# Expert blocks: gather by channel quarters, and a 32x32 block transpose on VectorE in place of TensorE transposes

## The chip, the cores and the metric

The kernel runs on one core of a Trainium2 chip. The metric is device microseconds of one execution, from three runs of the kernel before: 2274.1, 2275.79 and 2278.2 us, median 2275.79. Smaller is better. The engines have short names in the profile: PE is TensorE, DVE VectorE, ACT ScalarE, POOL GpSimd, SP SyncE.

## The reference

Two layers work on x of 4 sequences x 512 positions x 512 channels, in float32. Each layer has a first half (a WKV gate, then a token mixer: a Mamba2 block in layer 0, causal attention in layer 1) and a second half (a second WKV gate, then a feed-forward part: a mixture of experts in layer 0, a ternary FFN in layer 1); each half is added to x. The change lies in the mixture of experts:

```
logits = x @ gate_w.T + gate_b
top_vals, top_idx = jax.lax.top_k(logits, TOP_K)          # 2 of 8 experts
routing = jax.nn.softmax(top_vals, axis=-1)
for e in range(E):
    h = x @ w1[e].T + b1[e]                               # 512 -> 2 * 512
    x_glu, x_lin = h[:, 0::2], h[:, 1::2]
    y = x_glu * jax.nn.sigmoid(1.702 * x_glu) * (x_lin + 1.0)
    out = out + (y @ w2[e].T + b2[e]) * jnp.sum(routing * (top_idx == e), axis=-1)[:, None]
```

## The kernel before

The kernel is written in a tile framework: its scheduler puts the instructions of each engine in one order, and each engine then works through its own queue in that order, waiting on semaphores. The stages follow each other and overlap at their edges: the first WKV gates (0 to some 42 us), the Mamba2 block (to some 660 us), the experts (659 to 1134 us), attention (to about 2000 us), and the last FFN.

**Routing.** The gated rows of all 2048 tokens are written to a DRAM tensor `rows_h` (a row of 512 floats per token). The function `route` (L527) ranks the experts for every token and counts, with a triangular matrix `tri_lt` as matmul weight (L553), the place of each token within its expert; it also builds `toks`, a 128x128 table of tokens by place. `order_blocks` (L648 to L707) then makes blocks of 128 tokens of one expert: a matmul with `toks` gives the token of each lane of each block, and a few small DVE operations turn it into row indices, `idx_h` to gather with and `idx_o` to scatter with, and into the expert of a block, `eb`. It is called twice. The first call (L1433), before the last sequence is routed, orders 17 blocks (`NEARLY`); the second (L1525) orders the rest. 39 blocks are possible, 37 always run (`ALWAYS`), and the last two sit under a condition; 37 ran in the profiled execution.

**A block.** Class `Experts` does one block per round (`round`, L864), as a pipeline over three blocks:

- `fetch` (L766): one indirect DMA from POOL's queue (L770) gathers 128 rows of 2048 bytes into `hb` (128 partitions x 512 channels, three buffers). Fetches run `LOOK` = 3 blocks ahead, and a new one needs the buffer that a flip has freed.
- `flip` (L776): four PE transposes of 128x128 into a PSUM tile `pfl` (L782), and an ACT copy (L784) to `hT` (channels on partitions, two buffers).
- `first_half` (L806): four matmuls `pg` (L811), a bias add on DVE (`g`, L816), a tanh on ACT; four matmuls `pn` (L822), three DVE operations (L826 for g, L828 and L829 for u).
- `finish` (L832): four PE transposes `pyt` (L835) of u and an ACT pass to `yT` (L837).
- `down` (L840): four matmuls `po` (L844), a bias add to `o` (L849) and an indirect DMA that scatters the rows (L850).

A float32 matmul shows as two records in the profile, so a group of four has eight. PE's order in a steady round is pg of block i, pyt and po of earlier blocks, pfl of block i + 1, pn of block i.

**Weights.** `w1` lies in DRAM as `w1x`, laid out on the host (`_lay_out`, L1951) so that partition p of contraction part k holds channel 128 k + p. SP's queue loads each expert's halves ahead of the block.

**What stands beside it.** Between the rounds the program issues pieces of the next layer's WKV gates: scans of 1.2 us each on DVE (L259, L265), divisions, and ACT activations with table loads between them. At the edge to the stage before, the last Mamba2 work is still there: a multiply of y and the gate z on POOL (L1214), and a DVE operation `rs` (L1242) that waits for it. At the kernel's start POOL makes constants (iotas, triangular masks) and the skip multiplies (L957), while DVE runs the first WKV scans.

Of the kernel before, what the change touches and what calls it, by code (L numbers as in the profile page):

```python
# [18 lines left out]
P = 128  # L19
B, T, C = 4, 512, 512  # L20
NC = C // P
# [9 lines left out]
E, I = 8, 512  # L31
# [13 lines left out]

HEADS, GROUPS, KVC = 16, 4, 128
HPG = HEADS // GROUPS
SCALE = KVC ** -0.5
MASKED = -1.0e30

# [33 lines left out]
def block_kernel(ctx: ExitStack, tc: tile.TileContext, a: dict, out: bass.AP):  # L84
    nc = tc.nc
# [60 lines left out]
    def ps_tp(name):  # L146
        return ps.tile([P, 512], F32, tag="tp", name=name, bufs=2)
# [263 lines left out]
    def gated(l, b, xb, pool, part=slice(0, T), **kw):  # L411
# [25 lines left out]
    tri_lt = rt.tile([P, P], F32, name="tri_lt")  # L437
    nc.gpsimd.affine_select(out=tri_lt, in_=ones, compare_op=ALU.is_gt, fill=0.0, base=0,
                            pattern=[[1, P]], channel_multiplier=-1)
# [34 lines left out]
    e_nq = count("e_nq", [[NQ, E]])  # L474
    v_id = count("v_id", [[1, 1]], 1)

    v_lo = rt.tile([P, 1], F32, name="v_lo")
    v_e = rt.tile([P, 1], F32, name="v_e")
# [48 lines left out]
    def route(lg, b, fine, pool, **kw):  # L527
# [22 lines left out]
            yield  # L550
        pc = ps_tp("pcnt")
        mm_ = m.rearrange("p t e -> p (t e)")
        nc.tensor.matmul(pc[:, :n], lhsT=tri_lt, rhs=mm_, start=True, stop=True)  # L553
# [86 lines left out]


    taken = rt.tile([P, 1], F32, name="taken")
    idx_h = rt.tile([P, NBLK], I32, name="idx_h")
    idx_o = rt.tile([P, NBLK], I32, name="idx_o")
    eb = rt.tile([1, NBLK + 1], I32, name="eb")
    in_use = eb[:, NBLK:]
# [1 line left out]
    def order_blocks(lo, hi):  # L648

        n = hi - lo  # L650
        cv = rt.tile([P, 1], F32, tag="cv", name="cv")
        nc.vector.tensor_tensor(jk, sel, cnt[:, (N2 if lo else N2 - NT), :], ALU.mult)
        nc.vector.tensor_reduce(cv, jk, AX.X, ALU.add)
        use = rt.tile([P, 1], F32, tag="use", name="use")
        if lo == 0:
            nc.vector.scalar_tensor_tensor(use, v_lo, float(P), cv, ALU.add, ALU.is_le)
        else:
            nc.vector.tensor_tensor(use, v_lo, cv, ALU.is_lt)
            nc.vector.tensor_tensor(use, use, taken, ALU.subtract)
        pi = ps_tp("pidx")  # L660
        rank = rt.tile([P, 1], F32, tag="vrank", name="vrank")
        if lo == 0:
            nc.tensor.matmul(pi[:, P : P + 1], lhsT=tri_lt, rhs=use, start=True, stop=True)
            nc.vector.tensor_copy(rank, pi[:, P : P + 1])
        else:

            two = rt.tile([P, 2], F32, tag="two", name="two")
            nc.vector.tensor_tensor(jk, sel, cnt[:, NT, :], ALU.mult)
            nc.vector.tensor_reduce(rank, jk, AX.X, ALU.add)
            nc.vector.tensor_scalar(two[:, 0:1], v_lo, rank, use, ALU.is_lt, ALU.mult)  # L670
            nc.vector.tensor_tensor(two[:, 1:2], use, two[:, 0:1], ALU.subtract)
            nc.tensor.matmul(pi[:, P : P + 2], lhsT=tri_lt, rhs=two, start=True, stop=True)
# [7 lines left out]
            nc.vector.scalar_tensor_tensor(  # L680
                rank, pi[:, P : P + 1], two[:, 0:1], rank, ALU.mult, ALU.add
            )
        if lo == 0:
# [8 lines left out]
        gf = tmp.tile([P, NBLK], F32, tag="th", name="gf")  # L692
        nc.vector.tensor_scalar(gf[:, :n], pi[:, :n], NROW - 2.0, None, ALU.add)
        nc.vector.tensor_copy(idx_h[:, lo:hi], gf[:, :n])
        low = tmp.tile([P, NBLK], I32, tag="th", name="low")
        nc.vector.tensor_scalar(
            low[:, :n], idx_h[:, lo:hi], T - 1, (B - 1) * T, ALU.bitwise_and, ALU.bitwise_xor
        )
        nc.vector.tensor_scalar(
            idx_h[:, lo:hi], idx_h[:, lo:hi], 1, (B - 1) * T,  # L700
            ALU.logical_shift_right, ALU.bitwise_and,
        )
        nc.vector.tensor_tensor(idx_h[:, lo:hi], idx_h[:, lo:hi], low[:, :n], ALU.bitwise_xor)
        ef = tmp.tile([1, NBLK], F32, tag="th", name="ef")
        nc.vector.tensor_scalar(ef[:, :n], pi[0:1, 2 * P : 2 * P + n], E - 1.0, None, ALU.add)
        nc.vector.tensor_copy(eb[:, lo:hi], ef[:, :n])
        nc.vector.tensor_copy(idx_o[:, lo:hi], pi[:, :n])  # L707

    class Experts:
# [56 lines left out]
        def fetch(self, i):  # L766
            if i >= self.known or i in self.hb:
                return
            hb = self.sm.tile([P, C], F32, tag="hb", name="hb", bufs=3)
            nc.gpsimd.indirect_dma_start(  # L770
                out=hb, out_offset=None, in_=rows_h[: (B if i >= NEARLY else B - 1) * T, :],
                in_offset=bass.IndirectOffsetOnAxis(ap=idx_h[:, i : i + 1], axis=0),
            )
            self.hb[i] = hb

        def flip(self, i):  # L776
            if i in self.hT or i not in self.hb:
                return
            hb = self.hb[i]
            pt = ps_tp("pfl")  # L780
            for k in range(NC):
                nc.tensor.transpose(pt[:, k * P : (k + 1) * P], hb[:, k * P : (k + 1) * P], ident)  # L782
            hT = self.sm.tile([P, NC, P], F32, tag="hT", name="hT", bufs=2)
            nc.scalar.copy(hT.rearrange("p k t -> p (k t)"), pt)  # L784
            self.hT[i] = hT

        def weights(self, i, early=False):
# [764 lines left out]
    with att as ph:  # L1552
# [15 lines left out]
            )  # L1568
            return wd

        SQ, SLOTS = 32, 13
        QUAD = P // SQ
# [350 lines left out]
def _lay_out(n):  # L1923
# [24 lines left out]
        "gate_b": n["L0_ffn_gate_b"],  # L1948
    }
    by_part = lambda v: v.reshape(E, -1, P, v.shape[-1]).swapaxes(1, 2)  # L1950
    w1x = np.stack([by_part(t(w1[:, i::2, :])) for i in range(2)], 2)  # L1951
    got = {
        "cols": np.concatenate([cols[k] for k, _ in _COLS], 1),
        "rows": np.concatenate([np.asarray(rows[k]) for k, _ in _ROWS]),
# [35 lines left out]
```

## Time and profile before

| what | value |
|---|---|
| runs shown | 2274.1, 2275.79, 2278.2 us |
| the profiled execution's own time | 2278.28 us |
| its span (first to last instruction) | 2276.6 us |
| mean granted TensorE clock | 0.98 |
| PE busy | 2134.7 us |
| DVE busy | 1524.0 us |
| ACT busy | 972.2 us |
| POOL busy | 417.2 us |
| packets of under 512 B, of all | 14592 of 112452 |

The profile is of one execution. "Busy" is the time in which an engine has an instruction running. A group line names the source line, engine, operation, output and inputs, then busy us, mean ns of one, then the idle time of the engine just ahead of these instructions and what ended it. A timeline line gives start, duration, and in brackets the idle time before and what ended it. PE's matmuls overlap in the pipeline, so the distance between starts tells what a group costs. "Clock" is the share of full speed that TensorE was granted.

### The profile page before, as it was taken

How to read it: one execution, taken by the hardware profiler on the slowest of the kernel's cores; microseconds unless marked ns; L12 is line 12 of the kernel's file. 1: busy time of each engine (PE TensorE's matmuls, PEld its weight loads, DVE VectorE, ACT ScalarE, POOL GpSimd, SP SyncE). 2: the span in 40 equal slices, each digit the busy share in tenths (PEclk: the TensorE clock that was granted, in tenths of full speed). 3: DMA queues.
4: the chain of work that ended last, by engine and by line, in shares of the span. 5: the costliest groups of instructions: out<-in, count | busy, mean ns of one | idle time of the engine just before them, and what ended most of it. 6: DMA issues, size and time to landing. Idle time of an engine off the chain costs nothing. (4 is left out here: it accounts for less than half of the span.)

```text
span 2276.6 us, 23890 instructions
## 1 busy us (share of the span) xinstructions
PE 2134.7 (94%) x7528; PEld 1226.5 (54%) x7528; DVE 1524.0 (67%) x3041; ACT 972.2 (43%) x1900; POOL 417.2 (18%) x558
## 2 busy tenths in 40 slices
PE   2879999999999999999989999999999999999998
PEld 1545565555655444444444455555555555568887
DVE  8698989989642665566567766566667765456332
ACT  4476666766732233233254434333333333243222
POOL 4023232421332111111211111111111111100000
PEclk9889989999999999999999999999999999999999
DMA  7542341432523548978675566446545464441100
GB/s 261 169 141 75 102 158 66 153 121 65 186 76 136 190 164 298 341 273 277 209 249 179 172 191 186 139 138 190 167 143 158 139 196 142 131 184 38 37 19 20
DMA packets 112452, 357.38 MB, mean 157 GB/s; under 512 B 14592, under 2 KB 23168, under 8 KB 102912
## 3 DMA queue, kind: packets, MB, share of 16 engines
q1 hardware_dynamic: 87584, 277.26, 36.0%
q0 software_dynamic: 22432, 74.34, 11.1%
q10 hardware_dynamic: 2304, 4.20, 0.5%
q8 instruction: 62, 1.02, 0.2%
q14 instruction: 70, 0.57, 0.1%
HBM read 337.91 MB, written 108.00 MB: 196 GB/s over the span
## 5 line engine op out<-in xcount | busy, mean ns | idle before, releaser
L1661 POOL DMA_DIRECT2D turned<-turned x248 | 135.4, 552 | 713.7 <-DVE turned L1653 435.6
L1615 PE MATMUL pq<-h,wq 128*128 128x512 f32 x512 | 235.4, 597 | 2.0 <-DVE h L404 1.7
L1717 PE MATMUL pd<-cx,wd 128*128 128x512 f32 x512 | 223.3, 594 | 0.0
L128 ACT ACTIVATE pr<-psc,nmax 128x128 f32<-128x128 f32 (+3 forms) x256 | 134.7, 526 | 168.9 <-DVE nmax L1642 168.3
L1048 PE MATMUL pc<-h,wxb 128*128 128x512 f32 x320 | 148.6, 620 | 44.3 <-DVE h L1307 39.2
L1637 PE MATMUL psc<-kT,qT 128*128 128x128 f32 (+3 forms) x512 | 158.2, 442 | 14.5 <-ACT pr L128 14.5
L1702 PE MATMUL pctx<-pT,v 128*128 128x512 f32 (+3 forms) x512 | 153.3, 443 | 13.7 <-DMA pT<-turned 13.3
L1640 DVE TENSOR_TENSOR psc<-psc,mask 128x128 f32<-128x128 f32 x256 | 70.4, 283 | 140.5 <-PE psc L1637 140.3
L1717 PEld LDWEIGHTS pd<-cx,wd 128*128 128x128 f32 x512 | 96.5, 191 | 115.3 <-issue 110.1
L1702 PEld LDWEIGHTS pctx<-pT,v 128*128 128x128 f32 x512 | 98.1, 193 | 98.0 <-issue 67.0
L1615 PEld LDWEIGHTS pq<-h,wq 128*128 128x128 f32 x512 | 94.4, 192 | 100.9 <-issue 93.7
L811 PE MATMUL pg<-w,hT 128*128 128x512 f32 x296 | 136.0, 601 | 6.9 <-ACT hT L784 6.8
L844 PE MATMUL po<-w,yT 128*128 128x512 f32 x296 | 135.9, 600 | 6.2 <-ACT yT L837 6.2
L822 PE MATMUL pn<-w,hT 128*128 128x512 f32 x296 | 133.3, 592 | 0.0
L1725 DVE TENSOR_TENSOR xr<-xr,pd 128x512 f32<-128x512 f32 x64 | 43.8, 685 | 126.6 <-PE pd L1717 126.6
L1637 PEld LDWEIGHTS psc<-kT,qT 128*128 128x128 f32 x512 | 86.2, 192 | 73.6 <-ACT pr L128 31.1
L1048 PEld LDWEIGHTS pc<-h,wxb 128*128 128x128 f32 x320 | 61.8, 198 | 116.4 <-issue 74.5
L1642 DVE TENSOR_REDUCE nmax<-psc 128x1 f32<-128x128 f32 (+3 forms) x256 | 122.7, 480 | 1.9
L1653 DVE STREAM_TRANSPOSE turned<-pr 128x128 f32<-128x128 f32 x248 | 120.8, 498 | 1.4
L1710 ACT COPY cx<-pctx 128x512 f32<-128x512 f32 x64 | 37.2, 581 | 187.5 <-PE pctx L1702 187.5
L1119 PE MATMUL pz<-wzt,h 128*128 128x512 f32 x256 | 115.2, 598 | 0.3 <-ACT st L1220 0.3
L1267 PE MATMUL po<-wot,yT 128*128 128x512 f32 x256 | 115.2, 604 | 0.0
(343 smaller groups left out, 4198.0 us busy)
## 6 DMA issues: line engine op xcount, KB each, us to landing
w<-in_w1x SPq DMA_DIRECT2D x76, 1024.0 KB
turned<-turned POOLq DMA_DIRECT2D x248, 208.0 KB, 3.9
pT<-turned SPq DMA_DIRECT2D x62, 832.0 KB
w<-in_w2x SPq DMA_DIRECT2D x38, 1024.0 KB
wb<-in_b1x SPq DMA_DIRECT2D x38, 512.0 KB
lm<-cs SPq DMA_DIRECT2D x32, 512.0 KB
kt<-in_fT SPq DMA_DIRECT2D x62, 256.0 KB
ek<-ek SPq DMA_DIRECT2D x62, 256.0 KB
```

The source lines that it names most:

```text
L128: nc.scalar.activation(*args, **kw)
L811: nc.tensor.matmul(pg, lhsT=hT[:, k, :], rhs=self.w1[s][0][:, k, :], start=(k == 0), stop=(k == NC - 1))
L822: nc.tensor.matmul(pn, lhsT=hT[:, k, :], rhs=self.w1[s][1][:, k, :], start=(k == 0), stop=(k == NC - 1))
L844: nc.tensor.matmul(po, lhsT=yT[:, j, :], rhs=self.w2[s][:, j, :], start=(j == 0), stop=(j == NI - 1))
L1048: nc.tensor.matmul(pc, lhsT=wxb[:, k, m * P : (m + 1) * P], rhs=h[:, k, :], start=(k == 0), stop=(k == NC - 1),)
L1615: nc.tensor.matmul(pq, lhsT=u.wq[:, k, i * KVC : (i + 1) * KVC], rhs=u.h[:, k, :], start=(k == 0), stop=(k == NC - 1),)
L1637: nc.tensor.matmul(psc[:, :n], lhsT=qT[:, qi * P : n], rhs=u.kT[:, :n], start=True, stop=True)
L1642: nc.vector.tensor_reduce(nmax, psc[:, :n], AX.X, ALU.max, negate=True)
L1653: nc.vector.transpose(blocks[:, :, 3 * qi : 4 * qi + 1, :].rearrange("p c k j -> p k c j"), pr)
L1661: nc.gpsimd.dma_start(out=d[:, :, r].rearrange("c i s -> i c s"), in_=blocks[r * SQ : (r + 1) * SQ].rearrange("i c k j -> i c (k j)"),)
L1702: nc.tensor.matmul(pctx[:, kj * P :].rearrange("p (q r j) -> p q r j", r=QUAD, j=SQ), lhsT=u.v[:, kj, :], rhs=pT[:, :, 4 * kj : 10 + kj : ...
L1717: nc.tensor.matmul(po, lhsT=dense_w[u.g][:, i, m * P : (m + 1) * P], rhs=u.ctxT[i], start=(i == 0), stop=(i == HPG - 1),)
```

## The change

The gather becomes four indirect DMAs per block. The rows in DRAM are seen as 8192 quarters of 128 channels (512 bytes). Partition p takes channel quarter p // 32, and the r-th DMA brings, for the 32 tokens 32 r to 32 r + 31, one quarter to each of four groups of 32 partitions: `hb` is now [128, 4, 128]. One DVE transpose, which turns each 32x32 block within its group of 32 partitions, then gives `hT` with channels on partitions and all 128 tokens side by side. The channel on partition p of part k is thus not 128 k + p but 128 (p // 32) + 32 k + p % 32, and the host lays out `w1x` in that order. PE's transposes and ACT's copy go.

The indices are four times as many: `order_blocks` makes a widened copy of `toks` (each group of 32 columns repeated four times, 128x512, on DVE), four matmuls with it, and arithmetic on [128, 4, n] instead of [128, n], and then puts the quarter's number in the low two bits. The number is made once, by an iota on POOL and a DVE operation. `tri_lt` is dropped: `route` uses `tri_gt`, which the Mamba2 block has already (tokens of a tile are then counted from the other end), and `order_blocks` uses `tri_le` and subtracts the diagonal, `use`. `v_lo` and `v_e` become columns of one tile.

```
-    idx_h = rt.tile([P, NBLK], I32, name="idx_h")
+    idx_h = rt.tile([P, QUAD, NBLK], I32, name="idx_h")
+    quarter = rt.tile([P, 1], I32, name="quarter")
+    nc.gpsimd.iota(quarter, pattern=[[1, 1]], base=0, channel_multiplier=1)
+    nc.vector.tensor_scalar(
+        quarter, quarter, 5, QUAD * (B - 1) * T, ALU.logical_shift_right, ALU.bitwise_xor
+    )
...
+        wide = tmp.tile([P, QUAD, QUAD, SQ], F32, tag="th", name="wide")
+        nc.vector.tensor_copy(
+            wide,
+            toks.rearrange("p (r j) -> p r j", r=QUAD).unsqueeze(2).to_broadcast([P, QUAD, QUAD, SQ]),
+        )
+        for r in range(QUAD):
+            nc.tensor.matmul(
+                pi[:, 3 * P + r * n : 3 * P + (r + 1) * n],
+                lhsT=wide[:, r].rearrange("p q j -> p (q j)"),
+                rhs=of[:, :n], start=True, stop=True,
+            )
...
+        nc.vector.tensor_scalar(
+            low, ih, 2, QUAD * (T - 1), ALU.logical_shift_left, ALU.bitwise_and
         )
         nc.vector.tensor_scalar(
+            ih, ih, 1, QUAD * (B - 1) * T, ALU.logical_shift_left, ALU.bitwise_and
         )
+        nc.vector.tensor_tensor(ih, ih, low, ALU.bitwise_xor)
+        nc.vector.tensor_tensor(
+            ih, ih, quarter.unsqueeze(2).to_broadcast([P, QUAD, n]), ALU.bitwise_xor
+        )
...
-            hb = self.sm.tile([P, C], F32, tag="hb", name="hb", bufs=3)
-            nc.gpsimd.indirect_dma_start(
-                out=hb, out_offset=None, in_=rows_h[: (B if i >= NEARLY else B - 1) * T, :],
-                in_offset=bass.IndirectOffsetOnAxis(ap=idx_h[:, i : i + 1], axis=0),
-            )
+            hb = self.sm.tile([P, QUAD, NC * SQ], F32, tag="hb", name="hb", bufs=3)
+            quarters = rows_h[: (B if i >= NEARLY else B - 1) * T, :].rearrange(
+                "r (q c) -> (r q) c", q=QUAD
+            )
+            for r in range(QUAD):
+                nc.gpsimd.indirect_dma_start(
+                    out=hb[:, r, :], out_offset=None, in_=quarters,
+                    in_offset=bass.IndirectOffsetOnAxis(ap=idx_h[:, r, i : i + 1], axis=0),
+                )
...
-            pt = ps_tp("pfl")
-            for k in range(NC):
-                nc.tensor.transpose(pt[:, k * P : (k + 1) * P], hb[:, k * P : (k + 1) * P], ident)
             hT = self.sm.tile([P, NC, P], F32, tag="hT", name="hT", bufs=2)
-            nc.scalar.copy(hT.rearrange("p k t -> p (k t)"), pt)
+            nc.vector.transpose(
+                hT.rearrange("p k (r j) -> p r k j", r=QUAD), hb.rearrange("p r c -> p (r c)")
+            )
...
-    by_part = lambda v: v.reshape(E, -1, P, v.shape[-1]).swapaxes(1, 2)
-    w1x = np.stack([by_part(t(w1[:, i::2, :])) for i in range(2)], 2)
+    by_part = lambda v: v.reshape(E, -1, P, v.shape[-1]).swapaxes(1, 2)
+    by_quad = lambda v: v.reshape(E, QUAD, NC, SQ, -1).swapaxes(2, 3).reshape(E, P, NC, -1)
+    w1x = np.stack([by_quad(t(w1[:, i::2, :])) for i in range(2)], 2)
```

More of the change, by code (lines that the diff above doesn't have):

```diff
@@ L47 @@
 HPG = HEADS // GROUPS
+SQ = 32
+QUAD = P // SQ
 SCALE = KVC ** -0.5
@@ L435, in block_kernel @@
                             pattern=[[1, E], [-1, E]], channel_multiplier=0)
-    tri_lt = rt.tile([P, P], F32, name="tri_lt")
-    nc.gpsimd.affine_select(out=tri_lt, in_=ones, compare_op=ALU.is_gt, fill=0.0, base=0,
-                            pattern=[[1, P]], channel_multiplier=-1)
     sel = rt.tile([P, E], F32, name="sel")
@@ L475, in block_kernel @@
     v_id = count("v_id", [[1, 1]], 1)
-    v_lo = rt.tile([P, 1], F32, name="v_lo")
-    v_e = rt.tile([P, 1], F32, name="v_e")
+    v_both = rt.tile([P, 2], F32, name="v_both")
+    v_lo, v_e = v_both[:, 0:1], v_both[:, 1:2]
     jk = rt.tile([P, E], F32, name="jk")
@@ L552, in route @@
         mm_ = m.rearrange("p t e -> p (t e)")
-        nc.tensor.matmul(pc[:, :n], lhsT=tri_lt, rhs=mm_, start=True, stop=True)
+        nc.tensor.matmul(pc[:, :n], lhsT=tri_gt, rhs=mm_, start=True, stop=True)
         nc.tensor.matmul(pc[:, n : 2 * n], lhsT=ones, rhs=mm_, start=True, stop=True)
@@ L662, in order_blocks @@
         if lo == 0:
-            nc.tensor.matmul(pi[:, P : P + 1], lhsT=tri_lt, rhs=use, start=True, stop=True)
-            nc.vector.tensor_copy(rank, pi[:, P : P + 1])
+            nc.tensor.matmul(pi[:, P : P + 1], lhsT=tri_le, rhs=use, start=True, stop=True)
+            nc.vector.tensor_tensor(rank, pi[:, P : P + 1], use, ALU.subtract)
         else:
@@ L671, in order_blocks @@
             nc.vector.tensor_tensor(two[:, 1:2], use, two[:, 0:1], ALU.subtract)
-            nc.tensor.matmul(pi[:, P : P + 2], lhsT=tri_lt, rhs=two, start=True, stop=True)
+            nc.tensor.matmul(pi[:, P : P + 2], lhsT=tri_le, rhs=two, start=True, stop=True)
             nc.tensor.matmul(pi[:, P + 2 : P + 3], lhsT=ones, rhs=two[:, 0:1], start=True, stop=True)
@@ L682, in order_blocks @@
             )
+            nc.vector.tensor_tensor(rank, rank, use, ALU.subtract)
         if lo == 0:
@@ L690, in order_blocks @@
         nc.tensor.matmul(pi[0:1, 2 * P : 2 * P + n], lhsT=v_e, rhs=of[:, :n], start=True, stop=True)
[L692 to L695, printed above, removed]
-        nc.vector.tensor_scalar(
-            low[:, :n], idx_h[:, lo:hi], T - 1, (B - 1) * T, ALU.bitwise_and, ALU.bitwise_xor
+        wide = tmp.tile([P, QUAD, QUAD, SQ], F32, tag="th", name="wide")
[9 more added lines that the diff above has]
+            )
+        ih = idx_h[:, :, lo:hi]
+        gf = tmp.tile([P, QUAD, n], F32, tag="th", name="gf")
+        nc.vector.tensor_scalar(
+            gf, pi[:, 3 * P : 3 * P + QUAD * n].rearrange("p (r n) -> p r n", r=QUAD),
+            NROW - 2.0, None, ALU.add,
+        )
+        nc.vector.tensor_copy(ih, gf)
+        low = tmp.tile([P, QUAD, n], I32, tag="th", name="low")
+        nc.vector.tensor_scalar(
+            low, ih, 2, QUAD * (T - 1), ALU.logical_shift_left, ALU.bitwise_and
         )
         nc.vector.tensor_scalar(
-            idx_h[:, lo:hi], idx_h[:, lo:hi], 1, (B - 1) * T,
-            ALU.logical_shift_right, ALU.bitwise_and,
-        )
-        nc.vector.tensor_tensor(idx_h[:, lo:hi], idx_h[:, lo:hi], low[:, :n], ALU.bitwise_xor)
+            ih, ih, 1, QUAD * (B - 1) * T, ALU.logical_shift_left, ALU.bitwise_and
+        )
+        nc.vector.tensor_tensor(ih, ih, low, ALU.bitwise_xor)
+        nc.vector.tensor_tensor(
+            ih, ih, quarter.unsqueeze(2).to_broadcast([P, QUAD, n]), ALU.bitwise_xor
+        )
         ef = tmp.tile([1, NBLK], F32, tag="th", name="ef")
@@ L1569, in load_dense @@
             return wd
-        SQ, SLOTS = 32, 13
-        QUAD = P // SQ
+        SLOTS = 13
         turned = [mp.tile([P, QUAD, SLOTS, SQ], F32, name=f"turned{i}") for i in range(2)]
```

## The prediction

> **What bounds the kernel now.** The page's first parts come first: where TensorE (PE) is busy throughout, only what shortens PE's own work, or a wait of PE, can move the end. PE is busy 94% of the span, and the chain that ended last runs over it.
>
> ```profile
> PE 2134.7 (94%) x7528; PEld 1226.5 (54%) x7528; DVE 1524.0 (67%) x3041; ACT 972.2 (43%) x1900; POOL 417.2 (18%) x558
> ...
> PE 38%; DVE 7%; DMA 3%; ACT 1%; issue 0%; SPq 0%; DVEq 0%; ACTq 0%
> ```
>
> An average hides stages, so the windows come next (columns: length, then busy us and instructions of PE, PEld, DVE, ACT, POOL, then clock, DMA share, GB/s): the kernel's start, and the expert stage with its edges.
>
> ```profile
> 0.00:45.00 45.00, 3.16 (x5) 1.68 (x6) 39.02 (x67) 23.08 (x33) 13.24 (x31) 1.00 0.80 283
> 660.00:1140.00 480.00, 455.61 (x1348) 221.25 (x1348) 263.46 (x396) 143.79 (x213) 93.75 (x108) 0.98 0.66 230
> ```
>
> The first 42 us wait for VectorE (DVE, 39 of 45 us busy). The expert stage is PE's: 456 of 480 us, and DVE, with 263, is not its bound on average. Now the groups that the change removes, and its POOL fetch:
>
> ```profile
> L782 PE MATMUL pfl<-ident,hb 128*128 128x128 f32 x148 | 23.2, 281 | 3.3 <-DMA hb<-rows_h,idx_h 3.3
> L784 ACT COPY hT<-pfl 128x512 f32<-128x512 f32 x37 | 21.5, 581 | 40.6 <-PE pfl L782 40.6
> L770 POOL DMA_INDIRECT hb<-rows_h,idx_h x37 | 40.3, 1088 | 203.1 <-PE pfl L782 193.0 <-DVE eb L706 7.3 <-issue 2.8
> ```
>
> Busy time is not time on PE's path: 23.2/37 = 0.63 us per block counts overlapping ends. The distance of starts counts. The timeline of one undisturbed round:
>
> ```profile
> 885.30 0.60 PE L782 MATMUL pfl<-ident,hb 128*128 128x128 f32 x4
> 885.74 3.60 PE L822 MATMUL pn<-w,hT 128*128 128x512 f32 x8
> 889.17 3.60 PE L811 MATMUL pg<-w,hT 128*128 128x512 f32 x8
> 892.60 0.60 PE L835 MATMUL pyt<-ident,u 128*128 128x128 f32 x4
> 893.04 3.60 PE L844 MATMUL po<-w,yT 128*128 128x512 f32 x8
> 896.48 0.60 PE L782 MATMUL pfl<-ident,hb 128*128 128x128 f32 x4
> 896.91 2.31 PE L822 MATMUL pn<-w,hT 128*128 128x512 f32 x5
> ```
>
> A round is 896.91 - 885.74 = 11.17 us: three groups of 3.43, two of 0.43-0.44. Nothing else stands between, so a round without pfl is 10.74. But the stage also has PE stalls, one about every 4.2 rounds, beside the WKV work (scans, den, num, and ACT's table switches) that is interleaved with it. PE's timeline shows what ended them:
>
> ```profile
> 806.29 5.40 PE L811 MATMUL pg<-w,hT 128*128 128x512 f32 x8 [4.18 <-ACT hT L784]
> ...
> 998.09 3.70 PE L844 MATMUL po<-w,yT 128*128 128x512 f32 x8 [1.33 <-ACT yT L837]
> ```
>
> The six are at 806 (4.18), 854 (1.32), 902 (1.32), 950 (3.28, yT), 998 and 1044 (1.33 each, yT). After 4.18 the pg takes 5.40 instead of 3.60: the granted clock is half for one 3.41-us step from 807.5. The same step follows 950. No half step follows the 1.32 and 1.33 idles; each of the eight idles of 2.0 to 3.2 us on PE's timeline (at 77, 99, 131, 143, 660, 1134, 1157, 1616) has one.
>
> **Part by part**, against the profiled execution's own time, 2278.3 (2.5 above the median, so the forecast is that sum less 2.5). The compiled order of both kernels' instructions says what stands behind what.
>
> *Transposes off PE:* 37 x 0.43 = **-15.9** if PE stays the bound in every round.
>
> *The ACT copy goes*, 37 x 0.58 us. It ended the idle before pg at 806, 854 and 902. What is late next is u or yT.
>
> *One DVE transpose per block.* The trace has this form: attention's 128x512 STREAM_TRANSPOSE (L1653) takes 701 ns, its 128x128 one 300. Bounds: 0.70 (output as dense as there) and 4 x 0.30 = 1.20 (four separate pieces); I take 0.70, the nearer row, one instruction of the same tile. In the compiled order flip(i+2) stands right behind L828 of round i, before L829. So hT is a round early and PE does not wait for it; but L829, hence pyt(i), is 0.70 later, and so is the WKV work queued behind on DVE. In the round above L828 ends at 890.06, L829 would end at 891.5 instead of 890.79, and pyt starts at 892.60: hidden, with 1.1 left. If a 1.27-us scan stands ahead, the cover is gone.
>
> *At the six stalls* the chain from DVE through ACT to yT holds two flips, +1.4 at most. At 854, 998 and 1044 I take +1.3, so idles near 2.6, which by the row above draw the half clock: (5.40 - 3.60) = 1.8, less overlap 1.7. Three times 3.0: **+9.0** (bounds 0, if the flips slip into DVE's waits, and 9.3). 902 ended by hT goes: **-1.3** (-1.3 to +1.4). 950: in the compiled order yT comes ahead of a 1.28-us table load, 1.9 earlier, against 1.1 of flips: **-0.8** (-1.9 to +1.4). 806: its hT falls away, yet u comes through the same DVE block: **0** (-2.9 to +1.4).
>
> *Four gathers per block on POOL.* Back to back fetches start 1.28 us apart at 661.05 and 662.33 (0.94-0.97 plus 0.30 issue); 941/992/1480 is the minimum, median and maximum. Four and a scatter: 4 x 1.28 + 1.38 = 6.5 of 10.74 per round. It fits, and a block is fetched three rounds ahead, against landings of 3.2 to 9.2 us. Bounds of one gather's cost: 0.3 (a quarter of the bytes) and 1.78 (1.48 plus 0.30): at 1.78 POOL has 8.5 of 10.74, still no wait. The bytes are unchanged. The stage's DMA share is 0.66.
>
> *Start of the stage.* Before, POOL fetches at 659.51, after eb. Then two flips wait for landings (2.81 idle at 663.36). After: index work is longer by a wide DVE copy (0.69), four matmuls and small DVE operations, about 0.9; block 0 needs four gathers, +3.8 of issue, part of it covered by SSM work that the order now puts before pg(0). And 24 gathers (six blocks, 24 x 1.28 = 31 us) stand in POOL's queue before the SSM's y*zs multiply (L1214); DVE's next rs (L1242) waits for it, from about 681 to 694, and what is queued on DVE behind rs with it. The landing of pg(0) to pn(4) is set by that: **+3.0** (bounds 0 and +7).
>
> *Second ordering of blocks (L1525):* the wide copy 0.69, matmuls 0.9 and one flip stand in front of the DMA indices while PE runs low: **+2.2** (0 to 3).
>
> *Kernel's start.* The order there is reshuffled by iotas and the missing tri_lt: POOL's skip multiplies (L957, 0.6 to 1.46 each) now come before the iotas for place and e_nq, whose DVE copies stand ahead of the backward scan (L265) that ran at 12.08. DVE is the bound there: **+2.5** (0 to 3.5).
>
> Sum: -15.9 + 9.0 - 1.3 - 0.8 + 0 + 3.0 + 2.2 + 2.5 = **-1.3**, that is 2277.0 by the profiled execution, 2274.5 by the median; I write 2274.
>
> **Where the skill speaks against it.** Row: fetches take 0.94 to 1.48 us on POOL beside a DVE that is busy 263 of 480 us. The Trainium skill, "SBUF — State Buffer", section "A bandwidth-pool intuition that's wrong (but worth ruling out)", says that DVE copies that use both ports lock GpSimd out of writing descriptors, so that such a DMA of about 620 ns takes about 3100. By it a round would hold 5 x 3.1 = 15.5 us of POOL against today's 11.17, an estimate of about +130 over 30 rounds. The row has no such fetch among 37, and I go by the row.
> The Trainium skill, "TensorE: Matmul & The Clock Gate", section "What's actually happening", has the clock halve after an idle window of about 3.4 us, which would spare the 2.6-us idles (sum -6.4); the eight rows with idles of 2.0 to 3.2 disagree, and decide.
>
> **Rivals.**
> (B) *The full gain reaches the end.* For it: PE is 95% busy in the stage, and DVE has 217 us free. The flips slip into DVE's waits; 854, 998 and 1044 stay at 1.3; 806 and 902 shrink by 2.9 and 1.3; the starts cost 1 together: -15.9 - 4.2 + 1 = -19, 2257. Against: stalls were already ended by this chain. Chance 0.18.
> (C) *Slower: DVE's added 0.70 per round.* Place: the DVE-to-ACT chain at the six WKV stalls. Price: 1.4 of idle at each, and the half clock, 1.7, at the four that had none: 6 x 1.4 + 4 x 1.7 = 15.2. With +5 and +2.2 at the two orderings and +3.5 at the start: -15.9 + 25.9 = +10, 2286. It decides from the point where stalls, orderings and start cost 15.9 + 4.6 = 20.5. For it: the half-clock rows. Against: DVE's waits around the stalls, and hT's exit from ACT. Chance 0.27.
> (D) *POOL becomes the round's bound.* Decides from (10.74 - 1.38)/4 = 2.34 us a gather; at 2.7 a round is 12.2 against today's 11.17, +1.0 over 30 rounds: about 2307. Against: no fetch is over 1.48. Chance 0.04.
> (E) *The change doesn't do what it says:* the strided transpose costs 1.20 and pushes the flip behind WKV work, so that pg waits on DVE where it waited on ACT; the gain and 37 x 0.43 cancel: about +2, 2278. Chance 0.08.
> (A) The forecast, 2268 to 2279: chance 0.43.
>
> **How the numbers follow.** A measurement tells 0.2%, 4.55 us, from no change. A divides into faster 0.14, same 0.26, slower 0.03; B is faster; C and D are slower; E is same. Faster 0.14 + 0.18 = 0.32; same 0.26 + 0.08 = 0.34; slower 0.03 + 0.27 + 0.04 = 0.34. The range 2258 to 2288 leaves out half of B (0.09), the upper third of C (0.07) and D (0.04).
>
> **What would show it.** Right: pfl and the hT copy gone, rounds of 10.74, a DVE transpose of 0.70 x37, 148 gathers near 1 us, the 902 stall gone, idles of 2 to 3 with half-clock steps at three stalls, pg(0) later, and PE's first big group 2.5 later than 42.4. Wrong: idles of 1.3 unchanged (B), half-clock steps at every stall (C), gathers over 2.3 us or PE waiting on hb in the rounds (D), a flip over 1 us ahead of pg (E).

## The result and the profile after

The changed kernel takes 2297.26 us (median of 6 runs, 2293.26 to 2303.72); the kernel before, run beside it, 2275.46 (2272.76 to 2284.18). The ratio is 1.009, 95% interval 1.007 to 1.0109: **slower by 21.8 us**, outside the predicted range (2258 to 2288). The profiled execution of after is its slowest run, 2303.72 us with a span of 2301.9, 25.3 longer than the span of before.

The page's first and fifth part, after:

```profile
PE 2139.2 (93%) x7396; PEld 1219.7 (53%) x7396; DVE 1544.7 (67%) x3084; ACT 952.5 (41%) x1863; POOL 547.1 (24%) x669
...
L796 POOL DMA_INDIRECT hb<-rows_h,idx_h x148 | 172.0, 1162 | 150.0 <-DVE hT L807 99.6
...
L836 PE MATMUL pg<-w,hT 128*128 128x512 f32 x296 | 139.2, 613 | 7.4 <-DVE hT L807 6.4
```

The change did what it says. The `pfl` group and its ACT copy are gone (132 PE instructions fewer, the new index matmuls counted), 148 gathers of 1.16 us took the place of 37 fetches of 1.09, and PE waits for `hT` once only, 6.4 us at the stage's start. A steady round, in PE's timeline of after:

```profile
908.75 3.70 PE L847 MATMUL pn<-w,hT 128*128 128x512 f32 x8
912.29 3.60 PE L836 MATMUL pg<-w,hT 128*128 128x512 f32 x8
915.72 0.60 PE L860 MATMUL pyt<-ident,u 128*128 128x128 f32 x4
916.16 3.60 PE L869 MATMUL po<-w,yT 128*128 128x512 f32 x8
919.60 3.60 PE L847 MATMUL pn<-w,hT 128*128 128x512 f32 x8
923.03 3.60 PE L836 MATMUL pg<-w,hT 128*128 128x512 f32 x8
```

From pg to pg it is 923.03 - 912.29 = 10.74 us, against 11.17 before. So the gain per round is there, and the loss is somewhere else. To find it, each PE instruction of after is set beside the same one of before, and the difference of their starts is followed through the run: 0.8 us up to 60 us, **17.1 at 100 us**, 16.3 at 640 us, ahead of the expert stage, 16.4 at its last pn, 20.6 from 1700 to 2020 us, and from there it grows steadily to **25.1** at the end. The first rise and the last lie far from the expert blocks. The 4.2 us between, in attention, stay open: over the same stretch the traces of the other runs move by -3.4 (e4) to +4.1 (e12), so one trace cannot tell them from chance. The windows show the first one (length, then busy us and instructions of PE, PEld, DVE, ACT, POOL, clock, DMA share, GB/s). Before:

```profile
60.00:100.00 40.00, 35.64 (x101) 19.20 (x99) 28.72 (x56) 11.02 (x16) 1.33 (x1) 0.87 0.53 175
```

After:

```profile
60.00:100.00 40.00, 24.01 (x60) 11.39 (x59) 21.38 (x31) 8.10 (x11) 2.03 (x1) 0.81 0.54 179
```

PE loses 11.6 us of work in these 40, while DVE and ACT are idler too: all stand for the same reason. DVE's timeline of after names it:

```profile
65.30 0.66 DVE L282 TENSOR_TENSOR num<-num,eu 128x512 f32<-128x512 f32 x1
65.88 1.52 DVE L1088 SCALAR_TENSOR_TENSOR xc<-pc,cols,xc 128x511 f32<-128x511 f32 x2
84.23 0.43 DVE L245 TENSOR_SCALAR ek<-kt 128x512 f32<-128x512 f32 x1 [16.83 <-DMA kt<-in_fT]
84.57 14.52 DVE L1088 SCALAR_TENSOR_TENSOR xc<-pc,cols,xc 128x509 f32<-128x509 f32 x22
```

The operation `ek` of a WKV gate (its keys, loaded by SP into `kt`) stands ahead of 23 steps of the Mamba2 convolution (`xc`). Its load was issued at 64.21, behind three copies of FFN weights that SP had issued at 51.84, 57.68 and 58.24; 2816 KB each, within DRAM, for a stage that begins 1950 us later. SP's timeline of after, the last copy and the load:

```profile
58.24 0.59 SPq L1786 DMA_DIRECT2D ffd_d<-in_downT  x1
64.21 0.35 SPq L242 DMA_DIRECT2D kt<-in_fT  x1
```

DVE waits 16.8 us, and everything behind `ek` with it. In before the same `ek` (L243) stands behind those steps and runs at 93.79 without a wait:

```profile
93.79 0.42 DVE L243 TENSOR_SCALAR ek<-kt 128x512 f32<-128x512 f32 x1
```

PE's timeline of after shows the bill:

```profile
59.82 13.04 PE L1073 MATMUL pc<-h,wxb 128*128 128x512 f32 x30
85.46 8.43 PE L1073 MATMUL pc<-h,wxb 128*128 128x512 f32 x12 [12.61 <-DVE xc L1088]
97.28 5.96 PE L998 MATMUL pdt<-wxb,h 128*128 128x16 f32 x32 [3.39 <-DVE xc L1088]
```

12.61 us of idle, and the matmuls after it run slower (8.43 us for twelve records, 0.70 each, where the thirty ahead took 0.43): the granted clock is half from 77.9 to 91.6 us.

### The profile page after: what moved, and what is told of

It is laid out like the page before. It is cut to its first block, busy times and chain, and to the rows that moved or that the text cites. A ratio compares the mean times of both kernels' runs of the same rounds, so it can differ in the third digit from the quotient of the medians.

```text
span 2301.9 us, 23754 instructions
## 1 busy us (share of the span) xinstructions
PE 2139.2 (93%) x7396; PEld 1219.7 (53%) x7396; DVE 1544.7 (67%) x3084; ACT 952.5 (41%) x1863; POOL 547.1 (24%) x669
## 4 chain that ended last, share of the span: by engine, by line
PE 38%; DVE 7%; DMA 4%; ACT 1%; issue 0%; SPq 0%; POOL 0%; DVEq 0%; ACTq 0%
PE pd L1741 9%; PE pq L1639 6%; PE pctx L1726 5%; PE psc L1661 3%; DMA pT<-turned 3%; PE pv L1625 2%; PE pk L1617 2%; PE pfg L1843 2%; PE pfu L1843 2%; PE pfo L1843 2%; PE pfg L1844 2%; PE pfo L1844 2%; PE pfu L1844 2%; DVE turned L1677 1%; DVE nmax L1666 1%; DVE pr L1673 1%
## 5 line engine op out<-in xcount | busy, mean ns | idle before, releaser
L796 POOL DMA_INDIRECT hb<-rows_h,idx_h x148 | 172.0, 1162 | 150.0 <-DVE hT L807 99.6
L1661 PE MATMUL psc<-kT,qT 128*128 128x128 f32 (+3 forms) x512 | 158.5, 442 | 16.3 <-ACT pr L130 15.7
L1726 PE MATMUL pctx<-pT,v 128*128 128x512 f32 (+3 forms) x512 | 153.8, 444 | 14.5 <-DMA pT<-turned 14.2
L869 PE MATMUL po<-w,yT 128*128 128x512 f32 x296 | 140.8, 618 | 7.4 <-ACT yT L862 7.4
```

Source lines behind the costliest of these rows:

```text
L796: nc.gpsimd.indirect_dma_start(out=hb[:, r, :], out_offset=None, in_=quarters, in_offset=bass.IndirectOffsetOnAxis(ap=idx_h[:, r, i : i + ...
L869: nc.tensor.matmul(po, lhsT=yT[:, j, :], rhs=self.w2[s][:, j, :], start=(j == 0), stop=(j == NI - 1))
L1661: nc.tensor.matmul(psc[:, :n], lhsT=qT[:, qi * P : n], rhs=u.kT[:, :n], start=True, stop=True)
L1726: nc.tensor.matmul(pctx[:, kj * P :].rearrange("p (q r j) -> p q r j", r=QUAD, j=SQ), lhsT=u.v[:, kj, :], rhs=pT[:, :, 4 * kj : 10 + kj : ...
```

## The experiments

The theory: the loss is the wait of `ek` (some 16 us) plus a slower last FFN (some 4.5); the expert stage itself gained a little. The first rival: the loss lies in the expert stage or the gathers' traffic, and the two jumps are chance.

**e1, the quarter's number made late.** The only new work at the kernel's start is one iota and one DVE operation for `quarter`. They move into `order_blocks`; nothing else changes place on PE, ACT, POOL and SP, and on DVE `ek` falls back behind the convolution.

```
     quarter = rt.tile([P, 1], I32, name="quarter")
-    nc.gpsimd.iota(quarter, ...)
-    nc.vector.tensor_scalar(quarter, quarter, 5, ...)
...
         if lo == 0:
+            nc.gpsimd.iota(quarter, ...)
+            nc.vector.tensor_scalar(quarter, quarter, 5, ...)
```

> The changed kernel, with the two instructions that make the quarter's number (an iota on POOL, one operation on DVE) moved into the first ordering of blocks. In the compiled order nothing else moves but 23 conv steps of DVE past the ek operation (L245) that waits for a kt load. Theory (the loss is that operation standing in DVE's queue ahead of the conv steps): the 16.8-us DVE idle at 67 us and the 12.6-us PE idle at 73 us go, PE's offset to the kernel before at 100 us falls from 17 to about 1, time 2297 - 16 = 2281 (2277 to 2284). Rival (the expert stage lost the time: flips on DVE, gathers on POOL): no change within 3 us, 2294 to 2300.

Measured: 2281.5 us (12 runs; before beside it 2278.71; ratio 1.002, 1.0002 to 1.0038), 15.8 less than after (19.0 less, when each is taken from the kernel before that ran beside it). DVE's timeline of e1 has no wait left at this place:

```profile
66.17 16.62 DVE L1089 SCALAR_TENSOR_TENSOR xc<-pc,cols,xc 128x511 f32<-128x511 f32 x25
...
94.99 0.42 DVE L245 TENSOR_SCALAR ek<-kt 128x512 f32<-128x512 f32 x1
```

**e2, the two instructions alone, in the kernel before.** They write a column that nothing reads; the expert stage is as before.

```
-    idx_o = rt.tile([P, NBLK], I32, name="idx_o")
+    idx_o = rt.tile([P, NBLK + 1], I32, name="idx_o")
+    quarter = idx_o[:, NBLK:]
+    nc.gpsimd.iota(quarter, ...)
+    nc.vector.tensor_scalar(quarter, quarter, 5, ...)
```

> The kernel before, with the iota and the DVE operation added at the same place as in the change, writing a column that nobody reads: no gather, flip or index is changed. In the compiled order the ek operation then stands ahead of all conv steps of the first Mamba sequence. Theory: DVE idles some 16 to 18 us at 65 us and the time is 2275.5 + 17 = 2292 (2288 to 2296). Rival (the two instructions matter only together with the new expert work): within 2 us of the kernel before.

Measured: 2299.18 us (ratio 1.0091, 1.006 to 1.0122). Two instructions of 0.12 and 0.14 us, with no reader, cost 20 us, as much as the whole change. DVE's timeline of e2:

```profile
64.60 0.66 DVE L280 TENSOR_TENSOR num<-num,eu 128x512 f32<-128x512 f32 x1
82.56 0.43 DVE L243 TENSOR_SCALAR ek<-kt 128x512 f32<-128x512 f32 x1 [17.29 <-DMA kt<-in_fT]
82.90 16.86 DVE L1068 SCALAR_TENSOR_TENSOR xc<-pc,cols,xc 128x511 f32<-128x511 f32 x25
```

Here even the two steps that after still had ahead of `ek` are behind it, and PE's offset at 200 us is 19.95. It is not the instructions' own time but the order that the scheduler then chose.

**e3 and e4, the copies held back.** If `ek` waits because of the three copies in SP's queue, holding these takes the wait away with DVE's order as in after. A four-byte DMA into each target, from a tile that the first routing makes, holds each copy until then. e3 does so in after, e4 in before, as a control.

```
                 to, name = ((ffg_d, "gateT"), (ffu_d, "upT"), (ffd_d, "downT"))[b]
+                nc.sync.dma_start(out=to[0:1, 0:1], in_=is1[0:1, 0, 0:1])
                 nc.sync.dma_start(out=to, in_=a[name])
```

> The changed kernel, with the three FFN weight copies (2816 KB each, SP's queue, 52 to 58 us) held back until the first sequence is routed, near 290 us, by a 4-byte copy ahead of each. DVE's order is that of the changed kernel, with ek early. Theory (ek waits long because its kt load stands behind 8.4 MB of copies): DVE's idle at 67 us falls from 16.8 to some 2 us, time 2297 - 14 = 2283 (2278 to 2288), unless the copies disturb what is loaded near 290 us. Rival (ek waits for something else, a buffer or SP's own order): DVE's idle stays over 10 us, time within 3 us of 2297.

> Control for the run above: the kernel before with the same three copies held back. Both theories: no wait goes at 67 us, since ek stands behind the conv steps; time within 3 us of the kernel before, plus whatever the copies do near 290 us, which the run above has too.

Measured: e3 2285.66 (ratio 1.0038, 1.0021 to 1.0055), e4 2283.01 (1.0023, 1.0008 to 1.0038). In e3 `ek` runs at once, in the order of after:

```profile
66.47 1.52 DVE L1088 SCALAR_TENSOR_TENSOR xc<-pc,cols,xc 128x511 f32<-128x511 f32 x2
68.01 0.43 DVE L245 TENSOR_SCALAR ek<-kt 128x512 f32<-128x512 f32 x1
68.35 14.52 DVE L1088 SCALAR_TENSOR_TENSOR xc<-pc,cols,xc 128x509 f32<-128x509 f32 x22
```

So the wait needs both: `ek` early in DVE's order, and its load behind the copies. Held copies are no improvement of their own (the control is 4 us slower than before in the median, though its profiled execution was not), and the difference from e3 to e4, 2.7, is within the two intervals.

**e5 and e6, addresses.** In e1, PE's offset to before is -1.1 us at 2020 us and grows to 3.4 over the last FFN. There the operations and their order are the same, yet `pfu` and `pfg` are slower. What differs is where their operands lie: `tri_lt` went, `v_lo` and `v_e` share a tile, `idx_h` grew, and the compiled program places the later tiles on this side of SBUF 32 bytes lower (the weights `ffg` at byte 62400 of a partition, where they were at 62432, and `ffu` and `ffd` likewise). The rows that move through these matmuls, the gated halves of x, lie on the other side, at the same bytes in both programs, so of the two operands only the weights moved. e5 is e1 with the 32 bytes put back; e6 takes 32 bytes off before, by the shared tile alone.

```
-    quarter = rt.tile([P, 1], I32, name="quarter")
+    quarter = rt.tile([P, 16], I32, name="quarter")[:, :1]
```

```
-    v_lo = rt.tile([P, 1], F32, name="v_lo")
-    v_e = rt.tile([P, 1], F32, name="v_e")
+    v_both = rt.tile([P, 2], F32, name="v_both")
+    v_lo, v_e = v_both[:, 0:1], v_both[:, 1:2]
```

> The kernel with the quarter made late (2281.5 us), and 32 bytes per partition added to the quarter's tile, so that all later tiles, the FFN's weights among them, lie at the addresses that they have in the kernel before (they had moved down by 32 bytes). Instructions and orders on all engines are the same. Theory (the 704 gate and up matmuls of the last FFN run at 0.233 us instead of 0.227 because of where the weights lie): PE's offset to the kernel before stays flat from 2000 us to the end instead of growing by 4.5, time 2281.5 - 4.5 = 2277 (2273 to 2279). Rival (the slower matmuls come from something else, such as the state of the chip): 2281.5 within 2 us, and the growth is still there.

> The mirror: the kernel before with v_lo and v_e as columns of one tile, as the change has them, which moves the later tiles down by 32 bytes and leaves the order of all instructions as it was. Theory (addresses): the FFN's gate and up matmuls go from 0.227 to 0.233, +4.5 us over 2000 to 2260 us, time some 4.5 above the kernel before (2 to 7). Rival: no difference beyond 2 us.

Measured: e5 2276.04 us (before beside it 2278.99; ratio 0.999, 0.9975 to 1.0005), 5.5 below e1; e6 2280.79 (1.0011, 0.9992 to 1.003). PE's offset to before stays at -0.75 through the FFN in e5, and in e6 grows from -6.8 to -2.3. (The -6.8, with every engine's order as in before, shows how far two single profiles can lie apart.) The groups by line (ns: minimum, median, maximum, then first and last start) of before, after, e5 and e6, in this order:

```profile
L1819 PE MATMUL pfu<-h_hi,ffu x176: 387/389/397, 2012.5 to 2249.7; 128*128 128x512 f32 x176
```

```profile
L1843 PE MATMUL pfu<-h_hi,ffu x176: 389/396/398, 2033.1 to 2274.8; 128*128 128x512 f32 x176
```

```profile
L1844 PE MATMUL pfu<-h_hi,ffu x176: 389/389/399, 2011.8 to 2249.0; 128*128 128x512 f32 x176
```

```profile
L1819 PE MATMUL pfu<-h_hi,ffu x176: 392/394/397, 2005.7 to 2247.4; 128*128 128x512 f32 x176
```

The distance of starts is what PE pays: 0.2267 us a matmul in before and e5, 0.2333 in after, e1 and e6; 704 of them (pfg and pfu) x 0.0066 = 4.6 us, about the growth seen (4.5). e6's median alone, within its interval of no change, would not have shown it; the trace does. The two side effects thus explain the loss: 15.8 + 5.5 = 21.3 of 21.8 by the medians, 19.0 + 5.7 = 24.7 when each run is taken from the kernel before beside it; by the intervals such a difference is good to some 4 us. What is left, e5, is the change itself: **no difference that can be measured** (-5.7 to +1.1 us).

**e7 and e8, the flips in DVE's order.** Where did the 15.9 us of `pfl` go? PE's waits in the expert stage of e5 (brackets: idle before, and what ended it):

```profile
667.72 5.45 PE L837 MATMUL pg<-w,hT 128*128 128x512 f32 x8 [6.42 <-DVE hT L808]
...
752.64 0.38 PE L551 MATMUL pcnt<-rank,tri_gt 128*128 128x32 f32 x2 [1.74 <-DVE rank L546]
...
784.37 0.40 PE L694 MATMUL pidx<-of,toks 128*128 128x22 f32 x2 [2.14 <-DVE of L691]
812.18 1.09 PE L861 MATMUL pyt<-ident,u 128*128 128x128 f32 x4 [3.85 <-DVE u L855]
861.44 0.63 PE L861 MATMUL pyt<-ident,u 128*128 128x128 f32 x4 [3.21 <-DVE u L855]
882.11 3.70 PE L837 MATMUL pg<-w,hT 128*128 128x512 f32 x8 [0.74 <-DMA w<-in_w1x]
949.48 3.70 PE L870 MATMUL po<-w,yT 128*128 128x512 f32 x8 [2.24 <-ACT yT L863]
994.93 5.40 PE L870 MATMUL po<-w,yT 128*128 128x512 f32 x8 [2.23 <-ACT yT L863]
1042.09 5.40 PE L870 MATMUL po<-w,yT 128*128 128x512 f32 x8 [2.24 <-ACT yT L863]
```

The waits for `hT` at the WKV stalls became waits for u and yT, and three of before's 1.3 us (854, 998, 1044) are 2.2 to 3.2 now. Behind each of these three the granted clock is half for one step, from 862.4, 995.5 and 1043.3 (the last two show as 5.40 for a po). The wait at 949.48 is as long, 2.24, and has no such step. e7 asks whether the flip's place between L854 and L855 is to blame, and puts it behind both; e8 does every flip twice, to price it.

```
             u = sm.tile([P, I], F32, tag="u", name="u")
...
             nc.vector.tensor_tensor(u, g, u, ALU.mult)
...
+                with after(nc.vector):
+                    self.flip(i + 2)
```

```
             nc.vector.transpose(hT..., hb...)
+            nc.vector.transpose(hT..., hb...)
```

> The run with 32 bytes added, and DVE's flip of block i + 2 put behind the second u operation (u times g) of round i instead of ahead of it. Theory (the flip's 0.63 us stand in the chain from pn over u to pyt and yT that ends the six stalls): 0.6 less at each of the stalls, and at the ordering of blocks, -3 to -5 us against that run, 2273. Rival (DVE's queue is full of WKV work around the stalls, so the flip only changes places with it): within 1.5 us of that run.

> The run with 32 bytes added, and every flip done twice on DVE (the second writes the same values again): the price of 0.63 us of DVE per round. Theory (it counts at the stalls and at the two orderings of blocks alone): six stalls by 1.3, half-clock steps at one or two more, some 3 at the orderings: +9 us against that run (+5 to +14). Rival 1 (DVE is the bound of every round): 37 x 0.63 = +23. Rival 2 (hidden): within 2 us.

Measured: e7 2276.76 (1.0002, 0.9984 to 1.002): no gain, the rival was right; the yT waits are 2.36 instead of 2.24. e8 2280.96 (1.0014, 0.9997 to 1.0031), 4.9 above e5. PE's waits in e8:

```profile
669.73 6.71 PE L840 MATMUL pg<-w,hT 128*128 128x512 f32 x8 [7.20 <-DVE hT L811]
...
816.38 1.09 PE L864 MATMUL pyt<-ident,u 128*128 128x128 f32 x4 [4.77 <-DVE u L858]
...
954.29 5.40 PE L873 MATMUL po<-w,yT 128*128 128x512 f32 x8 [2.71 <-ACT yT L866]
```

A second flip adds 0.8 at the start, 0.5 to 0.9 at a wait for u or yT, and nothing in an undisturbed round, which stays 10.74: of 37 flips only those at the stalls and at the start are paid, by this trace.

**e9 and e10, ACT's order at the yT stalls.** In the compiled order of before and after, yT of these rounds stands behind ACT's table load and logarithm of a WKV gate. ACT's timeline of before, ahead of the wait at 998:

```profile
995.11 1.28 ACT L124 ACT_TABLE_LOAD   x1
996.41 1.15 ACT L124 ACTIVATE rec<-rec,tiny 128x1024 f32<-128x1024 f32 x1
997.46 0.58 ACT L837 ACTIVATE yT<-pyt 128x512 f32<-128x512 f32 x1
```

Holding the gate's pieces behind ACT's last instruction as well as DVE's puts yT and the next tanh ahead. e9 is e5 with that, e10 is before with that.

```
                 if moe.i < ALWAYS - NT + 1:
-                    with after(nc.vector):
+                    with after(nc.vector, nc.scalar):
                         send()
                         pump(1 + moe.i % 2)
```

> The run with 32 bytes added (2276.0 us), with one edit more: the pieces of WKV gate work issued between rounds also come after the round's last ACT instruction, so that in ACT's order yT and th stand ahead of the logarithm's table load and its two 1.1-us passes. Theory (the changed kernel's rounds have their full 0.44-us gain, and what eats it is the idles of 2.2 to 3.9 us with half-clock steps behind ACT's table block): the 2.24-us idles fall below 0.7 and their half-clock steps go, 5 to 12 us less, 2268 (2264 to 2271). Rival (DVE's queue, not ACT's, ends these idles, so another wait takes their place): within 2 us of 2276.

> Control: the kernel before with the same edit of the gate work's place. Theory (the table block is what ends its 1.33-us idles too, but no half-clock steps stand behind those): some 4 to 6 us less than the kernel before, 2273, and so the change, with its side effects taken out, is then 4 to 8 us ahead (2268 against 2273), more than the 3 us without the edit. Rival (the stalls have nothing to do with how much the change gains): the distance of the two stays 3 us.

Measured: e10 **2261.58 us** (6 runs, 2253.15 to 2264.93; before beside it 2275.79; ratio 0.9938, 0.9925 to 0.995), 14.2 faster, more than expected. ACT's timeline of e10 has yT ahead of the table load in the same round:

```profile
972.36 0.58 ACT L837 ACTIVATE yT<-pyt 128x512 f32<-128x512 f32 x1
...
975.91 1.28 ACT L124 ACT_TABLE_LOAD   x1
```

From 800 us on PE has no wait over 1 us in the stage, the rounds from 804 on are 11.18 but for two (11.39 and 11.28), and the half clock does not occur between 661 and 1112. Its profiled execution is its fastest: 17.6 us of its gain lie in the expert stage, 6.3 ahead of it, where the orders are those of before.

e9 gains nothing: 2277.59 (1.0011, 0.9996 to 1.0025). Its yT waits are gone too, and between 900 and 1120 us it gains 11 us on e5. But its profiled execution, its slowest (2293.07, 15.5 above the median), is already 8.9 us later than before's when the stage begins, and has a hole in the second round. In PE's timeline of e9:

```profile
704.20 5.38 PE L870 MATMUL po<-w,yT 128*128 128x512 f32 x6 [12.97 <-ACT yT L863]
```

PE's matmul for that yT had run at 690.63. Around it POOL works off one row of 24 gathers, from 669.29 to 699.76, ACT and DVE stand until just after. SP makes four issues at 685.69, 691.39, 698.45 and 703.40, which in e5 all fall between 673.64 and 677.36. In the trace's records SP does not wait there: 13 of its register operations between 683 and 703 take about 0.70 us each, where in e5 none between 660 and 720 takes over 0.18. POOL's and DVE's lines there:

```profile
698.82 0.94 POOL L797 DMA_INDIRECT hb<-rows_h,idx_h  x1 [0.30 <-issue]
699.78 1.28 POOL L1240 TENSOR_TENSOR y<-y,zs 128x512 f32<-128x512 f32 x1
...
701.93 0.15 DVE L1268 TENSOR_SCALAR rs<-rv 128x1 int32<-128x1 int32 x1 [9.79 <-issue]
```

This is the queue that the prediction named: y*zs behind 24 gathers, and DVE's `rs` behind y*zs. It does not explain why yT, on ACT, waits as well: e5 has the same row and its yT ran as soon as PE was done. Nor does the edit: up to 760 us of e5 every engine's order is the same in both. One profiled execution, and the slowest, cannot say whether the hole is in e9's median run; why e9 is no faster than e5 stays open.

**e11, another address.** e9 with 64 bytes put ahead of `ffd`, the weight of the FFN's third product, whose matmuls (pfo) are 0.2333 apart in before and after alike; the address then has the same remainder by 128 as the operand `hdhi`.

```
+        wf.tile([P, 16], F32, name="gap")
         wdn = wf.tile([P, NFF, C], F32, name="ffd")
```

> The same as the run with ACT's order edited, and a gap of 64 bytes ahead of the FFN's down weights. Theory (a float32r matmul of the FFN takes 0.227 us when weights and moving rows start at the same place in 128 bytes, as gate and up do in the kernel before, and 0.233 otherwise, as down does there): the 352 down matmuls go to 0.227, -2.3 us. Rival (the place in 128 bytes does not decide; it is another property of the addresses): down stays at 0.233, no difference.

Measured: 2277.42 (1.0003, 0.9982 to 1.0023); pfo goes from a median of 394 ns to 393, and PE gains 0.4 us over that stage. A miss: the weight's place by that rule is not what sets the pace. The hole is there again: 13.95 us, ended at 701.19.

**e12, the row of gathers broken up.** e9 with the fetches of the fourth to sixth block held behind what POOL and DVE were given before them. In POOL's order this moves eight gathers behind y*zs; the other engines' orders stay.

```
+            with after(*((nc.vector, nc.gpsimd) if 3 <= i < 6 else ())):
                 for r in range(QUAD):
                     nc.gpsimd.indirect_dma_start(
```

> The kernel of e9 with one thing moved: the fifth and sixth block's eight gathers stand behind the next multiplication of y by zs in POOL's order, so that 16 gathers and not 24 run in a row when the first routing is known, and y by zs comes some ten us sooner (8 x 1.25). All other engines' orders are those of e9. Theory: the idle of 12.97 us in e9's second round comes from the row of 24, during which every engine's next instructions came late (ACT, DVE and SP all stood from 691 to 703 with nothing to wait for, and were released within 5 us of the last gather). Then most of that idle goes, and the time is 2262 to 2269 us, that is e9's 2277.6 less 9 to 15. Rival: the idle has another cause that the row of gathers does not set, such as where the instructions lie; then the idle stays within 3 us of 13 at the same round and the time within 3 us of 2277.6.

Measured: 2275.69 (0.9993, 0.9973 to 1.0013). PE's timeline of e12:

```profile
685.91 2.84 PE L871 MATMUL po<-w,yT 128*128 128x512 f32 x6 [1.21 <-ACT yT L864]
...
716.18 1.11 PE L517 MATMUL pht<-ident,h_last 128*128 128x128 f32 x4 [5.91 <-DVE lg L508]
```

The hole shrinks from 12.97 to 1.21, but the eight gathers that were moved now hold the next `rs`, and a new wait of 5.91, for an operation behind that `rs` on DVE, appears where before had none. DVE's timeline of e12:

```profile
715.30 0.15 DVE L1269 TENSOR_SCALAR rs<-rv 128x1 int32<-128x1 int32 x1 [9.33 <-POOL rv L1263]
715.97 0.16 DVE L508 TENSOR_TENSOR lg<-pl,rows 128x8 f32<-128x8 f32 x1
```

The expected 2262 to 2269 was wrong. That the hole came with the row of 24 is not shown: the profiles of after, e1, e3 and e5 have the same row without a hole, and SP's slow operations are in e12 too, beside its row of 16 (676.9 to 685). How ACT, which waits for none of the gathers, came to stand stays open.

## Why the prediction was wrong

**Where it failed: the step "Kernel's start", +2.5 (0 to 3.5); the trace has 17.1 at 100 us and 16.3 at 640.** It compared the orders of the start, but followed them only as far as the first 42 us, to the backward scan. Up to 60 us the true difference is +0.8, less than the 2.5 that it took for this part. The operation that cost 16 us stood 20 us further down DVE's order, at a place where nothing was added, removed or edited: `ek` had changed sides with the convolution. In the trace of before that `ek` ran at 93.79 with no wait, so no row priced the wait; but its load's issue behind three copies of 2816 KB was in the trace, and the two orders side by side show the move. e1 (-15.8), e2 (+20) and e3 settle it.

**A term that was missing:** the last FFN, +4.5 to 5.5. The prediction treated what the change does not touch as unchanged. A shift of their weights by 32 bytes in SBUF slowed 704 matmuls by 3% (e5, e6). The trace of before had one hint, pfo at 394 ns beside pfu and pfg at 389, the same form on other tiles.

**The stage itself came out nearly as forecast, in part by luck:** the orderings cost 2.5 more than was said, and 950 gave back 1.9 more, where in this profile no half-clock step fell behind the wait of 2.24. The table takes the terms by the distance of pn's starts in e5 against before, one profile of each (the first at 673.01 against 671.06, the last at 1116.81 against 1119.30).

| term | predicted | measured |
|---|---|---|
| pfl off PE, 0.43 per round | -15.9 | -15.7 (36 distances x 0.4375) |
| stage start | +3.0 | +2.0 |
| first ten rounds, with the second ordering | +2.2 | +4.7 |
| stalls 854, 998, 1044 | +9.0 | +2.6, +2.6, +2.6 = +7.8 |
| 902 | -1.3 | -0.5 |
| 950 | -0.8 | -2.7 |
| 806 | 0 | +0.8 |
| last two rounds | none | +1.2 |
| sum | -3.8 | -2.5 (rounding of the parts aside) |

The step at the stalls was right in kind: idles of 1.3 grew past 2 and drew the half clock. The idles were 2.2 and 3.2 where 2.6 was said; e8 prices a flip at 0.5 to 0.9 there, where the prediction took 0.70 each. The second ordering was undersized: the wait for `rank` (0.30 before, 1.74 in e5) comes from DVE's order, and it brought a half-clock step that the sum did not have (from 753.2).

**The rivals.** B, the full gain, fell with the stalls. C (slower by DVE's 0.70) had the sign right, by luck: its 25.9 of costs in the stage and the start are 13 in e5, and the loss came from elsewhere. D is refuted for steady rounds: gathers are 1.16 us in the mean, 2.01 at most, and PE waits for none of them after the first. Of the queue at the stage's start, the wait is as the prediction said, DVE's `rs` at 692.74 in e5, 12.90 us idle ahead of it, but PE has no wait over 0.69 there; the +2.0 is the wait for the first flips. E fell: the strided transpose takes 0.70 (684 to 711 ns). One figure among the chances is off: the upper third of C is 0.09, not 0.07.

On the two rules weighed in the prediction: the longest of after's 148 gathers took 2.01 us beside a DVE that was busy 299 us of the 500 between 640 and 1140. The 3100 ns that the Trainium skill, "SBUF — State Buffer", section "A bandwidth-pool intuition that's wrong (but worth ruling out)", gives for such a DMA beside a DVE copy do not occur here. After idles of 2.23 to 2.24 us, e5 has half-clock steps at two of the three yT waits and after at two of three, and e10, whose waits from 800 us on are all under 1 us, has none; the window of some 3.4 us that the Trainium skill, "TensorE: Matmul & The Clock Gate", section "What's actually happening", calls idle need not be idle throughout by these rows.

## What to carry to other kernels

Compare the compiled order of every engine over the whole run, not only around the edit: an in-order queue can put a waiting instruction, here one whose load stood behind a bulk copy, ahead of work that PE needs, and two dead instructions were enough for 20 us. Before judging a change, take out its side effects (order at the start, addresses) in a kernel of its own; here the change itself was worth nothing that could be measured, and the loss came from its side effects. A stall that PE meets at regular places can be an order on another engine: here one word there (e10, 14 us, 2261.58) beat the edit that took 16 us of work off PE.

## What the runs showed of the hardware that was not expected

- The same float32r matmuls of 512 columns run 0.2267 or 0.2333 us apart as their weights lie 32 bytes higher or lower (before and e5 against after, e1 and e6); the moving rows lie at the same bytes. What about the weights' place decides is open; e11 rules out the simple rule that was tried for `ffd`.
- An idle of PE of 1.33 us never drew the half clock in the expert stage, one of 2.24 did in two cases of three (e5, and after alike), at a price of 1.7 us (a po of 5.40 instead of 3.70). The length of one idle does not decide alone: in before, idles of 0.84 and 1.09 us close together, at 566 and 568 us, have a step behind them, from 568.6.
- A gather of 128 rows of 512 bytes costs POOL as much as one of 2048 bytes: back to back 0.94 to 0.97 us each plus 0.30 to the next in both kernels, so four cost four times as much.
- In the profiles of e9 and e11 ACT, which waits for no gather, stood for some 12 us beside an unbroken row of 24 gathers, while SP's register operations took some 0.70 us. In after, e1, e3 and e5, with the same row, neither happened; why was not found.
